# Seven block products for layer 0's output projection, and one norm chain for its four row blocks

## The chip, the cores and the metric

The kernel runs on one core of a Trainium2 chip. The core has a matrix engine (TensorE, PE in the profile), a vector engine (VectorE, DVE), a scalar engine (ScalarE, ACT), GpSimd (POOL) and a queue of transfers issued by SyncE (SP). Each engine works through its own instructions in order; semaphores order them against each other. TensorE writes to PSUM[...].

The metric is the device time of one execution in microseconds, the median of several runs. Lower is better.

## The reference

The input x is 8 images of 512 channels and 32 x 32 = 1024 positions, all in float32. Two attention layers follow each other. Cut to what matters here, layer 0 is

```python
hn = group_norm(x, gn1_scale, gn1_bias)                  # 32 groups of 16 channels
qkv = einsum('bchw,oc->bohw', hn, w_qkv) + b_qkv
wgt = softmax((q * s).T @ (k * s))                       # 8 heads of 64 channels
a = einsum('bts,bcs->bct', wgt, v).reshape(b, c, h, w)
out = einsum('bchw,oc->bohw', a, w_proj) + b_proj        # the output projection
out = group_norm(out, gn2_scale, gn2_bias)
return x + out
```

Layer 1 takes this as its x: `qkv = w_qkv @ x` with row-normalized weights, divided by the root of its mean square over the channels, one-head attention over 1024 positions, an output matrix, and `(x + h) / sqrt(2)`.

## The kernel before, in words

**Tiles.** 512 channels are CI = 4 row blocks of 128 partitions, so an image is a tile of 4 x 1024 floats per partition. A matmul takes 128x128 weights and 128x512 moving data; the 1024 positions are two halves of 512 (HN). Seven buffers of one image's size ("slots") are handed out by name and given back (`big`, `slots.give`): x, the normed x, the values, the attention output `a`, the projected `o`, the turned probabilities `pT`. PSUM has three tiles of two banks (`wide`) and two of one bank (`bank`), used in turn.

**Order.** Every engine call goes through `InOrder`, which keeps the written order on each engine. The order of the work is thus that of the Python lines.

**A block** is one image. The loop `for b in range(B)` runs 32 softmax steps (4 pairs of heads, 8 query blocks). A step computes scores on TensorE, maximum and transpose on VectorE, exponentials on ScalarE, scaling on GpSimd, and moves the transposed probabilities into `pT` by four transfers on SP. TensorE fills its time with the projections of the next heads, and uses `pT` (`heads.values`) some steps later. `heads.turn` does the transpose and its four transfers.

**The end of the softmax** (lines 1003 to 1016). The next image's values (`project_v0`, 8 groups of 4 matmuls, handed out by `next(v0)`) are spread as filling: one group, the last values but one, the last transpose, `fetch("score", b)`, three groups, the last values, and then `finish_layer0`, which uses the other four groups.

**The projection and its norm** (`finish_layer0`, lines 527 to 584). For each row block j of the output and each half, 4 matmuls accumulate over the 4 row blocks of `a`: 32 matmuls. ScalarE writes the row with its bias to `o` (line 569). VectorE takes the statistics of each row (`bn_stats` twice, `bn_aggr`). `GroupNorm` averages them over groups of 16 channels by a small matmul with `gavg` (`pm`), subtracts, averages the variances by another (`pv`), takes an inverse root in 13 small VectorE steps (`rsqrt_steps`, line 190), and makes a scale `a` and an offset `c`. `apply` scales the row on ScalarE, `add` adds it to x on VectorE. Each row block has a chain of its own, staggered: rows are applied while later rows are projected, and the last two during v0's groups. The last block (`half`, `begun`) has half of the sums made during its softmax steps, since there is no next image to fill with.

**Layer 1** (`Layer1`) follows. `project` multiplies x by an upper triangular matrix `gram` (`py`, 20 matmuls; row cj needs rows 0 to cj of x), then `Seven` computes scores, values and weights. `Seven` (line 586) is a scheme of Strassen and Winograd: a product of 2 x 2 blocks from 7 block products in place of 8. Its left operands A11, A12, A22, S1 to S4 are blocks of the weights and sums of them, made once at the start and kept in DRAM (`far`); its right ones are blocks B of the data and sums T1 to T4 of them, which VectorE makes per block (`sum_x`). Two products share one PSUM tile and are drained together, mostly by additions on VectorE, into the four blocks of the result.

**Weights** do not all fit. They share three buffers, w_qk, w_v and w_p, and are fetched from DRAM anew in each block (`places`, `fetch`; SP's queue in written order): w_qk holds qk, then score; w_v holds v, then value; w_p holds proj, then gram. `fetch` waits until the readers of the former tenant are done. `prep_layer1` (line 899) makes the layer 1 weights and the transposed projection once, at the start.

Of the kernel before, what the change touches and what calls it, by code (L numbers as in the profile page):

```python
# [13 lines left out]
P = 128  # L14
# [38 lines left out]
def attention_blocks_kernel(  # L53
# [52 lines left out]
    def big(name, lead=CI):  # L106

        return slots.take([P, lead, CI * N // lead], name)
# [93 lines left out]
    def rsqrt(r, v, n, name):  # L202
# [300 lines left out]
    def out_terms(a, j, th, cis):  # L503
        hs = slice(th * HN, (th + 1) * HN)
        return [(near["proj"][:, ci, j * P : (j + 1) * P], a[:, ci, hs]) for ci in cis]
# [21 lines left out]
    def finish_layer0(b, h, xt, v0, o=None, begun=None):  # L527


        half = o is not None  # L530
        if not half:
            o = big(f"o_{b}")

        def project_out(j, th, pm):
            terms = out_terms(h.a, j, th, range(CI // 2, CI) if half else range(CI))
            if half and j in begun.pm:
                PE.matmul(pm[:, th, :], *terms[1], start=False, stop=True)
            else:
                run(matmuls(pm[:, th, :], terms))

        norms = {}

        def norm(j):
            st = small.tile([P, 2, 6], F32, tag="gn_st2", name=f"st2_{b}_{j}")
            mv = small.tile([P, 1, 2], F32, tag="gn_mv2", name=f"mv2_{b}_{j}")
            for k in range(2):
                gn_stats(st, o[:, j, :], k)
            VE.bn_aggr(mv[:, 0, :], st)
            norms[j] = GroupNorm(mv, 1, G2S + j, G2B + j, f"2_{b}_{j}")

        def apply(j):
            a, c = norms[j].coeffs()
            AC.activation(o[:, j, :], o[:, j, :], AF.Identity, bias=c, scale=a)

        def add(j):
            VE.tensor_add(xt[:, j, :], xt[:, j, :], o[:, j, :])

        for j in range(CI):
            pm = begun.pm[j] if half and j in begun.pm else wide(f"pp_{b}_{j}")
# [6 lines left out]
            if half:  # L566
                VE.tensor_add(o[:, j, :], o[:, j, :], pm.rearrange("p a f -> p (a f)"))
            else:
                AC.activation(o[:, j, :], pm.rearrange("p a f -> p (a f)"), AF.Identity, bias=col(BP, j))
# [5 lines left out]
        next(v0, None)  # L575
        fetch("gram", b)
        add(CI - 2)
        norms[CI - 1].means()
        next(v0, None)
        apply(CI - 1)  # L580
        add(CI - 1)
        run(v0)
        slots.give(f"a_{b}")
        slots.give(f"o_{b}")

    class Seven:

# [6 lines left out]

        half, drains = None, []

        def __init__(self, name, width, left, right, c, last, swap=False):
            self.name, self.width, self.left, self.right, self.swap = name, width, left, right, swap
            self.c, self.last = c, last

        def product(self, a, b, drain):
            first = Seven.half is None
# [22 lines left out]
        def steps(self):  # L625
            c, add, last = self.c, VE.tensor_add, self.last

            def c21(pm):
                add(c["21"], c["22"], pm)
                last("21")  # L630

            def both(pm):
                add(c["22"], c["22"], pm)
                last("22")
                add(c["12"], c["12"], pm)

            def c12(pm):
                add(c["12"], c["12"], pm)
                last("12")

            def c11(pm):
                add(c["11"], c["11"], pm)
                last("11")

            for a, b, drain in (
                (A11, "B11", lambda pm: AC.copy(c["11"], pm)),
                (S2, "T2", lambda pm: add(c["12"], c["11"], pm)),
                (S3, "T3", lambda pm: add(c["22"], c["12"], pm)),
                (A22, "T4", c21),
                (S1, "T1", both),  # L650
                (S4, "B22", c12),
                (A12, "B21", c11),
            ):
                self.product(a, b, drain)
                yield

    class Layer1:


# [1 line left out]

        def __init__(self, b, xt):
            self.b, self.xt = b, xt
            self.t12, self.t34 = (block.tile([P, 2, 2, HN], F32, tag="pb", name=f"t{k}_{b}") for k in (12, 34))
            self.e, self.sums = {}, {}

        def right(self, cols):

            first, second = cols, slice(HN + cols.start, HN + cols.stop)

            def operand(name, h):
                if name[0] == "B":
                    return self.xt[:, 2 * (name[1] == "2") + h, second if name[2] == "2" else first]
                tile_, k = {"T1": (self.t12, 0), "T2": (self.t12, 1), "T3": (self.t34, 0), "T4": (self.t34, 1)}[name]
                return tile_[:, k, h, cols]

            return operand

        def sum_x(self, j):

            xt, t12, t34 = self.xt, self.t12, self.t34
            m, (t1, t2) = j % 2, (slice(0, HN), slice(HN, N))
            if j < 2:
                VE.tensor_sub(t12[:, 0, m], xt[:, m, t2], xt[:, m, t1])
            else:
                VE.tensor_sub(t12[:, 1, m], xt[:, j, t2], t12[:, 0, m])
                VE.tensor_sub(t34[:, 0, m], xt[:, j, t2], xt[:, m, t2])
                VE.tensor_sub(t34[:, 1, m], xt[:, j, t1], t12[:, 1, m])

        def project(self):  # L690
            b, xt = self.b, self.xt
# [3 lines left out]
            for cj in range(CI):  # L695
                py = wide(f"py_{b}_{cj}")
                for th in range(2):
                    hs = slice(th * HN, (th + 1) * HN)
                    run(matmuls(py[:, th, :], [(near["gram"][:, ci, cj * P : (cj + 1) * P], xt[:, ci, hs]) for ci in range(cj + 1)]))
                self.sum_x(cj)  # L700
# [162 lines left out]
    PE.transpose(pcol, rows, ident[:NCOLS, :NCOLS])  # L863
    VE.tensor_copy(cols, pcol)
    VE.tensor_scalar_mul(bqs, cols[:, BQ : BQ + CI], QSCALE0)
    norm1.means()
    norm1.gn.coeffs()
    for ci in range(CI):
# [30 lines left out]
    def prep_layer1():  # L899
# [18 lines left out]
        for k, (name, w) in enumerate((("score", score), ("value", value))):  # L918
            pool, tag = ((block, "pb"), (prob, "p"))[k]
            s7 = [pool.tile([P, 4, 2, CH], F32, tag=tag, name=f"{name}7_{i}") for i in range(2)]  # L920
# [10 lines left out]
        done2 = big("done2", 2 * CI)  # L931
        gram, proj = done2[:, :CI, :], done2[:, CI:, :]

        VE.memset(gram, 0.0)
        for ci in range(CI):
# [8 lines left out]
        for name in ("w1_qk", "w1_vo", "rows_vp", "done1", "done2"):  # L944
            slots.give(name)
        fetch("proj", 0)

    prep_layer1()

# [5 lines left out]
    for b in range(B):  # L955
# [47 lines left out]
        v0 = iter(())  # L1003
        if more:
            v0_next = big(f"v0_{b + 1}", NT)
            v0 = project_v0(b + 1, hn_next, v0_next)
        next(v0, None)
        heads.values(STEPS // RG - 2)
        heads.turn()
        fetch("score", b)  # L1010
        for _ in range(3):
            next(v0, None)
# [63 lines left out]
```

## Time and profile before

| | us |
|---|---|
| median of 3 runs | 3366.11 |
| lowest, highest | 3365.45, 3367.4 |
| the profiled execution's own time | 3368.53 |
| its span, first to last instruction | 3366.4 |
| TensorE busy | 3310.3 (98%) |
| VectorE busy | 2093.1 (62%) |
| ScalarE busy | 1091.8 (32%) |
| GpSimd busy | 979.2 (29%) |
| mean granted TensorE clock | 0.996 of full |

The profile is one execution. Its views used here: the busy shares; the chain of work that ended last, followed back from the last instruction; the groups of instructions, with count, busy time, mean of one, and what ended the idle time before; the timeline of one engine; and windows, which give busy time of PE, PEld (weight loads), DVE, ACT, POOL, each with its number of records, then the granted clock of TensorE, the DMA share and GB/s for a stretch of time. Nearly every line of the kernel shows as L34, the helper that keeps the order, so groups are told apart by tile names: `pp` is the projection in PSUM, `pm` and `pv<-d,gavg` the norm's small matmuls, `pv<-v,hn` the next image's values, `py` the gram product, `p_u` layer 1's score products. A float32 matmul is two records.

### The profile page before, as it was taken

How to read it: one execution, taken by the hardware profiler on the slowest of the kernel's cores; microseconds unless marked ns; L12 is line 12 of the kernel's file. 1: busy time of each engine (PE TensorE's matmuls, PEld its weight loads, DVE VectorE, ACT ScalarE, POOL GpSimd, SP SyncE). 2: the span in 40 equal slices, each digit the busy share in tenths (PEclk: the TensorE clock that was granted, in tenths of full speed). 3: DMA queues.
4: the chain of work that ended last, by engine and by line, in shares of the span. 5: the costliest groups of instructions: out<-in, count | busy, mean ns of one | idle time of the engine just before them, and what ended most of it. 6: DMA issues, size and time to landing. Idle time of an engine off the chain costs nothing.

```text
span 3366.4 us, 36221 instructions
## 1 busy us (share of the span) xinstructions
PE 3310.3 (98%) x13329; PEld 1628.9 (48%) x13329; DVE 2093.1 (62%) x3175; ACT 1091.8 (32%) x1825; POOL 979.2 (29%) x852
## 2 busy tenths in 40 slices
PE   7999999999999999999999999999999999999799
PEld 3544544445444454444544445444454545444354
DVE  4595646956479454884449754596546956468653
ACT  2353123531145212451125412254123531145210
POOL 0253123521235112450224503254022521235111
PEclk9999999999999999999999999999999999999899
DMA  5486205752068410782118811287204852058500
GB/s 184 137 209 186 79 13 150 198 159 81 2 188 206 125 69 25 200 221 89 55 44 217 226 59 44 74 220 203 78 14 127 205 166 78 13 145 204 158 7 25
DMA packets 183239, 410.86 MB, mean 122 GB/s; under 512 B 27508, under 2 KB 27544, under 8 KB 176280
## 3 DMA queue, kind: packets, MB, share of 16 engines
q1 hardware_dynamic: 182944, 408.53, 42.8%
q8 instruction: 106, 1.74, 0.2%
q14 instruction: 69, 0.57, 0.1%
q10 hardware_dynamic: 120, 0.02, 0.0%
HBM read 114.32 MB, written 25.72 MB: 42 GB/s over the span
## 4 chain that ended last, share of the span: by engine, by line
PE 88%; DVE 7%; DMA 2%; ACT 1%; issue 1%; SPq 1%; DVEq 0%; ACTq 0%
PE po L34 26%; PE s L34 13%; PE pqk L34 13%; PE p_e_T L34 7%; PE p_e_B L34 5%; PE pv L34 5%; PE py L34 4%; PE pp L34 4%; PE p_u_T L34 3%; PE p_v_T L34 2%; PE p_u_B L34 2%; PE p_v_B L34 2%; DMA pT<-pb 2%; DVE s L34 1%; DVE rs L34 1%; DVE x L34 1%
## 5 line engine op out<-in xcount | busy, mean ns | idle before, releaser
L34 POOL TENSOR_SCALAR p<-p,tt 128x1024 f32<-128x1024 f32 x512 | 565.9, 1118 | 935.0 <-DVE tt L34 931.6
L34 ACT ACTIVATE p<-s,nm 128x1024 f32<-128x1024 f32 x512 | 565.5, 1109 | 839.9 <-DVE nm L34 800.2
L34 DVE TENSOR_REDUCE nm<-s 128x1 f32<-128x1024 f32 x512 | 602.3, 1218 | 174.4 <-PE s L34 173.7
L34 DVE STREAM_TRANSPOSE pb<-p 128x2048 f32<-128x2048 f32 x256 | 589.5, 2303 | 28.4 <-POOL p L34 18.7
L34 PE MATMUL s<-qk 64*128 64x512 f32 x2048 | 510.4, 602 | 0.0
L34 PE MATMUL po<-pT,v 128*64 128x256 f32 x4096 | 471.7, 383 | 3.7 <-DMA pT<-pb 3.3
L34 PE MATMUL pqk<-hn,qk 64*128 64x512 f32 (+1 forms) x2016 | 474.4, 591 | 0.0
L34 PE MATMUL po<-e,v 128*128 128x512 f32 x1024 | 450.8, 595 | 0.0
L34 PEld LDWEIGHTS po<-pT,v 128*64 128x64 f32 x4096 | 287.3, 137 | 216.9 <-ACT v L34 69.7
L34 PEld LDWEIGHTS pqk<-hn,qk 64*128 64x128 f32 (+1 forms) x2016 | 202.0, 187 | 252.1 <-issue 239.7
L34 POOL TENSOR_TENSOR u<-u,xy 128x512 f32<-128x512 f32 x64 | 79.0, 1273 | 817.9 <-DMA xy<-far_rinv 727.3
L34 PEld LDWEIGHTS po<-e,v 128*128 128x128 f32 x1024 | 192.2, 190 | 252.7 <-issue 245.5
L34 PEld LDWEIGHTS s<-qk 64*128 64x128 f32 x2048 | 194.6, 186 | 239.4 <-issue 234.5
L34 PE MATMUL pv<-v,hn 128*128 128x512 f32 x512 | 233.2, 604 | 1.4 <-ACT v L34 1.4
L34 PE MATMUL pp<-a,proj 128*128 128x512 f32 x480 | 217.4, 604 | 0.0
L34 DVE TENSOR_TENSOR e<-e,p_e_T 128x512 f32<-128x512 f32 x160 | 107.0, 685 | 145.0 <-PE p_e_T L34 142.8
L34 POOL TENSOR_TENSOR qk<-qk,v 128x512 f32<-128x512 f32 x124 | 158.2, 1276 | 84.2 <-ACT v L34 84.2
L34 ACT ACTIVATE e<-e,shift,rinv 128x512 f32<-128x512 f32 x128 | 100.9, 811 | 247.7 <-DVE e L34 247.7
L34 POOL TENSOR_TENSOR esum<-esum,e 128x512 f32<-128x512 f32 x96 | 121.5, 1267 | 163.9 <-ACT e L34 161.4
L34 PEld LDWEIGHTS pv<-v,hn 128*128 128x128 f32 x512 | 94.2, 191 | 111.2 <-issue 109.4
L34 PE MATMUL p_e_T<-s,t 128*128 128x512 f32 x320 | 147.8, 592 | 0.0
L34 DVE BATCH_NORM_STATS2 st<-o 128x6 f32<-128x512 f32 x64 | 41.0, 683 | 168.2 <-ACT o L34 168.2
(171 smaller groups left out, 3048.2 us busy)
## 6 DMA issues: line engine op xcount, KB each, us to landing
pT<-pb SPq DMA_DIRECT2D x1024, 256.0 KB, 4.5
hn<-in_x_dram SPq DMA_DIRECT2D x32, 512.0 KB, 5.8
x<-in_x_dram SPq DMA_DIRECT2D x32, 512.0 KB, 5.8
out_dram<-x SPq DMA_DIRECT2D x32, 512.0 KB, 3.9
score<-far_score SPq DMA_DIRECT2D x8, 1792.0 KB
value<-far_value SPq DMA_DIRECT2D x8, 1792.0 KB
qk<-far_qk SPq DMA_DIRECT2D x7, 2048.0 KB
proj<-far_proj SPq DMA_DIRECT2D x8, 1024.0 KB, 4.8
```

The costliest lines, as they stand in the source:

```text
L34: return lambda *args, **kw: self._pin(call(*args, **kw))
```

## The change

The output projection of the first seven blocks is computed by `Seven`: two units of 7 products, each product two matmuls, 28 in all. The weights' seven left operands are made in the set-up (`proj7`) and share the buffer w_qk with qk and score. `gram` stays in w_p from the start until the last block. The right operands' sums, formerly a method of `Layer1`, become a class `RightSide`, and are made for `a` in a slot of their own (`ta`): rows 0 to 2 ahead of the last values, row 3 after them. The bias is added in the drains of the first and the third product (`bpd` holds the difference of two biases). The statistics of all four rows go through one `GroupNorm` of width 4; rows are applied after it. The fetch of score moves behind the projection. The last block keeps its form under the name `finish_last`. In the set-up the transposition of the projection's weights moves ahead of the gram.

```diff
+    bpd = const.tile([P, 2], F32, name="bpd")
...
-        "proj": ("p", [P, CI, C]), "gram": ("p", [P, CI, C]),
+        "proj": ("p", [P, CI, C]), "gram": ("p", [P, CI, C]), "proj7": ("qk", [P, 7, 2, CH]),
...
+    class RightSide:
+        def __init__(self, xt, t12, t34):
+            self.xt, self.t12, self.t34 = xt, t12, t34
+
+        def sums(self, j):
+            xt, t12, t34 = self.xt, self.t12, self.t34
+            m, (t1, t2) = j % 2, (slice(0, HN), slice(HN, N))
+            if j < 2:
+                VE.tensor_sub(t12[:, 0, m], xt[:, m, t2], xt[:, m, t1])
+            else:
+                VE.tensor_sub(t12[:, 1, m], xt[:, j, t2], t12[:, 0, m])
+                VE.tensor_sub(t34[:, 0, m], xt[:, j, t2], xt[:, m, t2])
+                VE.tensor_sub(t34[:, 1, m], xt[:, j, t1], t12[:, 1, m])
...
     class Seven:
...
+            def c11_first(pm):
+                if self.bias:
+                    AC.activation(c["11"], pm, AF.Identity, bias=self.bias[0])
+                else:
+                    AC.copy(c["11"], pm)
+
+            def c22_first(pm):
+                if self.bias:
+                    VE.scalar_tensor_tensor(c["22"], pm, self.bias[1], c["12"], ALU.add, ALU.add)
+                else:
+                    add(c["22"], c["12"], pm)
...
             for a, b, drain in (
-                (A11, "B11", lambda pm: AC.copy(c["11"], pm)),
+                (A11, "B11", c11_first),
                 (S2, "T2", lambda pm: add(c["12"], c["11"], pm)),
-                (S3, "T3", lambda pm: add(c["22"], c["12"], pm)),
+                (S3, "T3", c22_first),
                 (A22, "T4", c21),
                 (S1, "T1", both),
                 (S4, "B22", c12),
...
+    def finish_layer0(b, h, rhs, xt, v0):
+        o, w = big(f"o_{b}"), near["proj7"]
+        st = small.tile([P, CI, 2, 6], F32, tag="gn_st2", name=f"st2_{b}")
+        mv = small.tile([P, CI, 2], F32, tag="gn_mv2", name=f"mv2_{b}")
+        norm = GroupNorm(mv, CI, G2S, G2B, f"2_{b}")
+
+        def unit(m):
+            c = {
+                f"{i + 1}{th + 1}": o[:, m + 2 * i, th * HN : (th + 1) * HN] for i in range(2) for th in range(2)
+            }
+            return Seven(
+                f"o_{b}_{m}", HN,
+                lambda k, hh: w[:, k, hh, m * P : (m + 1) * P], rhs.columns(slice(0, HN)), c, lambda which: None,
+                bias=(col(BP, m), bpd[:, m : m + 1]),
+            ).steps()
+
+        def stats(j):
+            for k in range(2):
+                gn_stats(st[:, j], o[:, j, :], k)
+
+        units = [unit(m) for m in range(2)]
+        for u in units:
+            next(u)
+
+        for j in range(CI // 2 + 1, CI):
+            rhs.sums(j)
+        for m, u in enumerate(units):
+            for k in range(6):
+                next(u)
+                if k == 3:
+                    stats(m + 2)
+            stats(m)
+        slots.give(f"a_{b}")
+        slots.give(f"ta_{b}")
+        fetch("score", b)
+        next(v0)
+        for j in range(CI):
+            VE.bn_aggr(mv[:, j, :], st[:, j])
+        norm.means()
+        next(v0)
+        a, c = norm.coeffs()
+        for j in range(CI):
+            AC.activation(o[:, j, :], o[:, j, :], AF.Identity, bias=c[:, j : j + 1], scale=a[:, j : j + 1])
+            VE.tensor_add(xt[:, j, :], xt[:, j, :], o[:, j, :])
+        run(v0)
+        slots.give(f"o_{b}")
...
-            if b + 1 < B:
+            if b + 1 == B - 1:
                 fetch("proj", b + 1)
...
+        for name, w, pool, tag in (("score", score, block, "pb"), ("value", value, prob, "p")):
+            operands(name, w, [pool.tile([P, 4, 2, CH], F32, tag=tag, name=f"{name}7_{i}") for i in range(2)])
+        slots.give("done1")
+        done2, done3 = big("done2", 2 * CI), big("done3", 2 * CI)
         gram, proj = done2[:, :CI, :], done2[:, CI:, :]
+        turn(wprow, proj, "p")
+        d3 = done3.rearrange("p (k h) c -> p k (h c)", k=2).rearrange("p k (i h c) -> p k i h c", h=2, c=CH)
+        operands("proj7", proj, [d3[:, k] for k in range(2)])
...
-        turn(wprow, proj, "p")
...
-        fetch("proj", 0)
+        fetch("gram", 0)
...
+            next(v0)
         heads.values(STEPS // RG - 2)
         heads.turn()
-        fetch("score", b)
-        for _ in range(3):
-            next(v0, None)
-        begun = None if more else OutBegun(b, heads)
+        if more:
+            fetch("proj7", b)
+            ta = big(f"ta_{b}").rearrange("p (k i) (h n) -> p k i h n", k=2, h=2)
+            rhs = RightSide(heads.a, ta[:, 0], ta[:, 1])
+            for j in range(CI // 2 + 1):
+                rhs.sums(j)
+            for _ in range(3):
+                next(v0)
+        else:
+            fetch("score", b)
+            begun = OutBegun(b, heads)
         heads.values(STEPS // RG - 1)
         slots.give(f"v0_{b}")
-        finish_layer0(b, heads, xt, v0, *(() if more else (o_last, begun)))
+        if more:
+            finish_layer0(b, heads, rhs, xt, v0)
+        else:
+            finish_last(b, heads, xt, o_last, begun)
```

`operands` is the code that made the seven left operands of score and value, now a function: four additions and subtractions on VectorE, three copies on GpSimd, two transfers to DRAM.

More of the change, by code (lines that the diff above doesn't have):

```diff
@@ L525, in __init__, with finish_last @@
                         PE.matmul(self.pm[j][:, th, :], lhsT, rhs, start=True, stop=False)
[L527 to L532, printed above, removed]
+    def finish_last(b, h, xt, o, begun):
         def project_out(j, th, pm):
-            terms = out_terms(h.a, j, th, range(CI // 2, CI) if half else range(CI))
-            if half and j in begun.pm:
+            terms = out_terms(h.a, j, th, range(CI // 2, CI))
+            if j in begun.pm:
                 PE.matmul(pm[:, th, :], *terms[1], start=False, stop=True)
@@ L558, in finish_layer0 @@
         for j in range(CI):
-            pm = begun.pm[j] if half and j in begun.pm else wide(f"pp_{b}_{j}")
+            pm = begun.pm[j] if j in begun.pm else wide(f"pp_{b}_{j}")
             project_out(j, 0, pm)
@@ L565, in finish_layer0 @@
                 add(j - 2)
[L566 to L569, printed above, removed]
+            VE.tensor_add(o[:, j, :], o[:, j, :], pm.rearrange("p a f -> p (a f)"))
             if j:
@@ L572, in finish_layer0 @@
             norm(j)
-        next(v0, None)
         apply(CI - 2)
-        next(v0, None)
         fetch("gram", b)
@@ L578, in finish_layer0, with columns, operand, __init__ @@
         norms[CI - 1].means()
-        next(v0, None)
         apply(CI - 1)
         add(CI - 1)
-        run(v0)
         slots.give(f"a_{b}")
         slots.give(f"o_{b}")
+    class RightSide:
[10 more added lines that the diff above has]
+                VE.tensor_sub(t34[:, 1, m], xt[:, j, t1], t12[:, 1, m])
+        def columns(self, cols):
+            first, second = cols, slice(HN + cols.start, HN + cols.stop)
+            def operand(name, h):
+                if name[0] == "B":
+                    return self.xt[:, 2 * (name[1] == "2") + h, second if name[2] == "2" else first]
+                tile_, k = {"T1": (self.t12, 0), "T2": (self.t12, 1), "T3": (self.t34, 0), "T4": (self.t34, 1)}[name]
+                return tile_[:, k, h, cols]
+            return operand
     class Seven:
         half, drains = None, []
-        def __init__(self, name, width, left, right, c, last, swap=False):
+        def __init__(self, name, width, left, right, c, last, swap=False, bias=None):
             self.name, self.width, self.left, self.right, self.swap = name, width, left, right, swap
-            self.c, self.last = c, last
+            self.c, self.last, self.bias = c, last, bias
         def product(self, a, b, drain):
@@ L663, in __init__ @@
             self.b, self.xt = b, xt
-            self.t12, self.t34 = (block.tile([P, 2, 2, HN], F32, tag="pb", name=f"t{k}_{b}") for k in (12, 34))
+            self.rhs = RightSide(xt, *(block.tile([P, 2, 2, HN], F32, tag="pb", name=f"t{k}_{b}") for k in (12, 34)))
+            self.right = self.rhs.columns
             self.e, self.sums = {}, {}
[L667 to L688, printed above, removed]
         def project(self):
@@ L699, in project @@
                     run(matmuls(py[:, th, :], [(near["gram"][:, ci, cj * P : (cj + 1) * P], xt[:, ci, hs]) for ci in range(cj + 1)]))
-                self.sum_x(cj)
+                self.rhs.sums(cj)
                 VE.tensor_mul(part if cj else acc, py.rearrange("p a f -> p (a f)"), xt[:, cj, :])
@@ L865, in attention_blocks_kernel @@
     VE.tensor_scalar_mul(bqs, cols[:, BQ : BQ + CI], QSCALE0)
+    VE.tensor_sub(bpd, cols[:, BP + 2 : BP + 4], cols[:, BP : BP + 2])
     norm1.means()
@@ L917, in prep_layer1, with operands @@
             AC.copy(value[:, ci, :], product(wv, [woT[:, o, :] for o in range(CI)], ci, 0, "pB"))
-        for k, (name, w) in enumerate((("score", score), ("value", value))):
-            pool, tag = ((block, "pb"), (prob, "p"))[k]
-            s7 = [pool.tile([P, 4, 2, CH], F32, tag=tag, name=f"{name}7_{i}") for i in range(2)]
+        def operands(name, w, s7):
             q = [[w[:, 2 * j : 2 * j + 2, i * CH : (i + 1) * CH] for j in range(2)] for i in range(2)]
@@ L930, in prep_layer1 @@
             SY.dma_start(out=far[name][:, 4:], in_=s7[1][:, :3])
-        done2 = big("done2", 2 * CI)
+        for name, w, pool, tag in (("score", score, block, "pb"), ("value", value, prob, "p")):
+            operands(name, w, [pool.tile([P, 4, 2, CH], F32, tag=tag, name=f"{name}7_{i}") for i in range(2)])
+        slots.give("done1")
+        done2, done3 = big("done2", 2 * CI), big("done3", 2 * CI)
         gram, proj = done2[:, :CI, :], done2[:, CI:, :]
+        turn(wprow, proj, "p")
+        d3 = done3.rearrange("p (k h) c -> p k (h c)", k=2).rearrange("p k (i h c) -> p k i h c", h=2, c=CH)
+        operands("proj7", proj, [d3[:, k] for k in range(2)])
         VE.memset(gram, 0.0)
@@ L940, in prep_layer1 @@
                 VE.tensor_scalar_mul(gram[:, ci, c0 + P :], pg[:, c0 + P :], 2.0)
-        turn(wprow, proj, "p")
         SY.dma_start(out=far["gram"], in_=gram)
         SY.dma_start(out=far["proj"], in_=proj)
-        for name in ("w1_qk", "w1_vo", "rows_vp", "done1", "done2"):
+        for name in ("w1_qk", "w1_vo", "rows_vp", "done2", "done3"):
             slots.give(name)
-        fetch("proj", 0)
+        fetch("gram", 0)
     prep_layer1()
@@ L1001, in attention_blocks_kernel @@
             heads.step(i, fill, early, later)
-        v0 = iter(())
         if more:
@@ L1006, in attention_blocks_kernel @@
             v0 = project_v0(b + 1, hn_next, v0_next)
-        next(v0, None)
+            next(v0)
         heads.values(STEPS // RG - 2)
         heads.turn()
-        fetch("score", b)
-        for _ in range(3):
-            next(v0, None)
-        begun = None if more else OutBegun(b, heads)
+        if more:
[9 more added lines that the diff above has]
+            begun = OutBegun(b, heads)
         heads.values(STEPS // RG - 1)
         slots.give(f"v0_{b}")
-        finish_layer0(b, heads, xt, v0, *(() if more else (o_last, begun)))
+        if more:
+            finish_layer0(b, heads, rhs, xt, v0)
+        else:
+            finish_last(b, heads, xt, o_last, begun)
         fetch("value", b)
```

## The prediction

> **What bounds the kernel now.** I read the page's busy shares and its chain first, then the groups, then TensorE's timeline around one output projection, then the load beside it. The first two name the bound:
>
> ```profile
> PE 3310.3 (98%) x13329; PEld 1628.9 (48%) x13329; DVE 2093.1 (62%) x3175; ACT 1091.8 (32%) x1825; POOL 979.2 (29%) x852
> PE 88%; DVE 7%; DMA 2%; ACT 1%; issue 1%; SPq 1%; DVEq 0%; ACTq 0%
> ```
>
> TensorE is busy 98% of the span and carries 88% of the chain. So a matmul that goes away is worth its time, if no engine makes TensorE wait in its place. These groups give the prices (behind the first bar: busy us and the mean ns of one record):
>
> ```profile
> L34 PE MATMUL pp<-a,proj 128*128 128x512 f32 x480 | 217.4, 604 | 0.0
> L34 DVE TENSOR_TENSOR u<-u,p_u_T 128x512 f32<-128x512 f32 x80 | 53.1, 680 | 43.6 <-PE p_u_T L34 42.5
> L34 DVE BATCH_NORM_STATS2 st<-o 128x6 f32<-128x512 f32 x64 | 41.0, 683 | 168.2 <-ACT o L34 168.2
> ```
>
> The 480 records of the projection are two per matmul (7 blocks x 32 + 16 in the last), and the 604 ns of a record overlap their neighbours. The true price comes from the timeline of TensorE, here block 1's projection and what follows (start, us, then the group):
>
> ```profile
> 725.51 14.00 PE L34 MATMUL pp<-a,proj 128*128 128x512 f32 x32
> 739.35 0.28 PE L34 MATMUL pm<-mv,gavg 128*128 128x1 f32 x2
> 739.49 3.68 PE L34 MATMUL pp<-a,proj 128*128 128x512 f32 x8
> 743.01 0.28 PE L34 MATMUL pv<-d,gavg 128*128 128x1 f32 x2
> ...
> 754.12 3.68 PE L34 MATMUL pv<-v,hn 128*128 128x512 f32 x8
> 757.92 0.38 PE L34 MATMUL pv<-d,gavg 128*128 128x1 f32 x2
> ...
> 765.71 0.38 PE L34 MATMUL pv<-d,gavg 128*128 128x1 f32 x2 [0.21 <-DVE d L34]
> 765.95 3.68 PE L34 MATMUL pv<-v,hn 128*128 128x512 f32 x8
> 769.47 17.33 PE L34 MATMUL py<-x,gram 128*128 128x512 f32 x40
> 786.63 1.88 PE L34 MATMUL p_u_B<-x,score 128*128 128x512 f32 x4
> ```
>
> The reader is to see three prices. **A matmul**: the 20 of py run from 769.47 to 786.63, 17.16 us, so 0.858 us each. **A small matmul of the norm**: from 739.49 to the next eight records of pp at 743.15 are 3.66 us, of which 4 x 0.858 = 3.43 are the big ones; 0.22 us remain. **The stage**: from the first pp to the first py 43.96 us here, and 43.69, 43.68, 43.68 and 43.68 us in the blocks at 319, 1131, 1942 and 2752 us; I take 43.7. It is made of 32 + 16 matmuls (4 groups of v0 follow the projection), 48 x 0.858 = 41.2; 8 small ones, 1.8; and 0.7 of waits for the norm, of which the row at 765.71 shows a piece.
>
> **The change, part by part.** All of it but the set-up falls into seven of the eight blocks; the last keeps its way.
>
> TensorE, per block. 28 product matmuls stand in place of 32: the new products have the form of layer 1's score products, which the rows show at 0.858 too (28 of them with a 1.7 us group between go from 786.63 to 812.45). One chain of the norm in place of four: 2 small matmuls for 8. New stage: 28 + 16 = 44 x 0.858 = 37.75; 2 x 0.22 = 0.44; waits, below, 0.1. Sum 38.3, so 5.4 us less per block: 3.4 from the products, 1.3 from small matmuls, 0.6 from waits.
>
> VectorE before the projection. The sums of rows 0 to 2 (5 subtractions, 0.60 us from start to start as in the rows of t<-x) are 3.1 us. VectorE did nothing from 709.95, its last transpose, to 733.83. They wait only until the values of the last group but one leave their buffer (711.4), and end near 714.6; nothing is queued behind them but the sums of row 3. Cost 0; without this cover they would cost 3.1.
>
> Row 3's sums come after the last values. Count from the end of these, 725.5 = 0: ScalarE writes row 3 by 0.6, the three subtractions end at 1.3, 1.9 and 2.5. The two first products (A11 x B11 of both units, no sums) keep TensorE until 3.43; the first use of a row-3 sum is at 4.3. Cover 3 us, cost 0.
>
> VectorE during the products: 3 sums, 14 drains (680 ns), 8 statistics (683 ns): 25 x 0.65 = 16 us within 24 us of TensorE. A pair of products takes 3.43 us, its drains at most 3 adds and 2 statistics, 3.3 us; three PSUM tiles rotate, so a pair may lag by two before TensorE waits. Cost 0. ScalarE drains two first products in place of four 128x1024 rows: less.
>
> The norm's tail is the one place where the change adds a wait. The products end at 24.0; I count anew from there. Two last adds to 1.3, two statistics to 2.6, four aggregates at 0.2 to 3.4. TensorE's first v0 group ends at 3.43, so the mean matmul waits 0 to 0.3; I take 0.1, since the steps of the trace start within 0.05 of their release. Mean and three small steps end at 4.7, while the second v0 group runs to 7.1. Then the variance matmul, 17 small steps of 0.194 (743.32 to 746.56 in block 1) to 10.7, ScalarE's row 1.24 to 12.0, the first add 1.22 to 13.2. The two last v0 groups hold TensorE until 4 x 3.43 + 0.44 + 0.1 = 14.3, when py wants row 0. Margin 1.1 us. Rows 1, 2, 3 are ready 1.2 us apart, py takes 1.7, 3.4 and 5.2 us per row. Cost 0; each us by which this chain is longer than counted past 1.1 costs 1 us per block. From above: if VectorE trails by a whole pair, 3 us, 1.9 us per block.
>
> Transfers. The proj7 load (1792 KB) stands on SP's queue where the score load stood, same size, same buffer, same release. What is new is that the projection needs it at once. Landing of the score load before (window of the DMA, last two columns DMA share and GB/s), in block 1 and in block 4, the tightest:
>
> ```profile
> 713.22 1.04 SPq L34 DMA_DIRECT2D score<-far_score  x1
> 722.50:723.00 0.50, 0.50 (x8) 0.33 (x6) 0.00 (x0) 0.50 (x1) 0.00 (x0) 1.00 0.07 29
> 723.00:723.50 0.50, 0.50 (x8) 0.31 (x6) 0.00 (x0) 0.03 (x1) 0.00 (x0) 1.00 0.00 0
> 1939.50:1940.00 0.50, 0.50 (x8) 0.29 (x6) 0.00 (x0) 0.00 (x0) 0.00 (x0) 1.00 0.19 61
> 1940.00:1940.50 0.50, 0.50 (x8) 0.34 (x6) 0.00 (x0) 0.00 (x0) 0.00 (x0) 1.00 0.00 0
> ```
>
> The last packets are in at 723.0 and 1940.0; the projection starts at 725.51 and 1941.84: 2.5 and 1.8 us to spare, 2.4 to 4.5 in the others. [...]By the row the cost is 0[...]; I take 0, and the range holds the rest. The score load moves behind the last product, at 24; alone it took 7 us in block 0 (307.6 to 315), so it lands near 32 and is read after py, at 24 + 14.3 + 17.2 = 55. On SP only the value load is queued behind its wait, and that waits for v0's end at 38 anyway. The gram load per block and seven of eight proj loads go; no TensorE wait hung on them: 0.
>
> Set-up, once: 4 VectorE and 3 GpSimd steps near 0.7 to 1.1 us, 1792 KB written, the 16 transposes moved ahead of the gram. VectorE was idle from 96 to 100 and from 101 to 108; with the steps it is ready near 103, and TensorE wants a bank back only at 110. Moved transposes: 1.8 us either way. The extra bias column on the start's chain: 0.2. Cost 0.2; without the cover 5.
>
> **Sum.** 7 x 5.4 = 37.8, less 0.2: 37.6. The profiled execution took 3368.5 us (span 3366.4 and 2.1 around it), 2.4 over the runs' median of 3366.1. It would come to 3330.9, the median to 3328.5.
>
> **Rivals.**
>
> The tail is longer: norm chain or load exposed by 1 to 4 us per block. For it: margins of 1.1 and 1.8 us. Against: both were counted from rows of the same forms. Time 3335 to 3356; at 2 us, 3342.
>
> Slower: proj7 lands late. A stall that long also costs clock. The last block shows it: TensorE idle for up to 5.8 us, and
>
> ```profile
> 3180.00:3185.00 5.00, 0.00 (x0) 0.00 (x0) 3.22 (x15) 1.24 (x1) 0.00 (x0) 0.50 0.32 135
> 3185.00:3190.00 5.00, 4.26 (x7) 2.20 (x8) 3.26 (x22) 0.31 (x1) 0.00 (x0) 0.50 0.00 0
> 3190.00:3195.00 5.00, 5.00 (x12) 2.17 (x12) 4.04 (x5) 0.93 (x1) 0.00 (x0) 0.96 0.00 0
> ```
>
> a granted clock of 0.50, and 19.4 us for the py that takes 17.2 elsewhere: 2.2 us more. [...]By the row a stall then costs itself and 2.2[...]; the gain of 5.4 is used up at 3.2[...] us.[...] The load would have to land 5 to 8 us later than the score load of the same size did in the same place. At 6 us late the time is 3328.5 + 7 x 8.2 = 3386.
>
> It does nothing: the gain comes back in a later stage, as where the softmax of blocks 3 and 4 waits for pT transfers (they stand on the chain at 1383 to 1421 and 1908 to 1923). Against: the waits of TensorE for pT come to 3.3 us in the whole span. Time 3360 to 3370.
>
> **How the numbers follow.** All hidden 0.85 (3325 to 3332); tail exposed 0.10; nothing 0.02; slower 0.03. Measurement tells 0.2% (6.7 us) from no change; below 3359.4 is faster: 0.95, same 0.02, slower 0.03. The range takes in the first case, 1 us per block more from fewer waits below and 1.7 us per block of exposed tail above: 3321 to 3340.
>
> **What would show it.** TensorE records of the output group fall by 7 x 8 = 56, small ones by 7 x 12 = 84. First product to first py: 38.3 us. Right: the first product starts with no wait for DMA, the clock stays at 1.00, and py starts with no wait for VectorE or 0.3 at most. Wrong: a wait of TensorE on proj7's load, or of py on x, times seven.

## The result, and the profile after

| | before | after |
|---|---|---|
| median, us | 3366.76 | 3327.27 |
| lowest, highest | 3365.45, 3368.5 | 3324.93, 3328.1 |
| the profiled execution, us | 3368.53 | 3326.53 |
| its span | 3366.4 | 3324.7 |
| mean granted TensorE clock | 0.996 | 0.997 |

After to before is 0.9881, with a 95% interval of 0.9864 to 0.9898: 39.5 us less, where 37.6 were forecast. Each median is of four runs.

The page of the kernel after, its busy shares and its chain:

```profile
PE 3270.4 (98%) x13189; PEld 1608.1 (48%) x13189; DVE 2127.5 (64%) x2893; ACT 1069.8 (32%) x1811; POOL 981.4 (30%) x855
PE 86%; DVE 6%; DMA 5%; SPq 2%; issue 1%; ACT 0%; DVEq 0%; POOL 0%; POOLq 0%; ACTq 0%
```

TensorE is 39.9 us less busy and still 98% busy, so the work that went was on the path and nothing has taken its place. The chain goes through transfers of `pT` more often than before (DMA 5% for 2%), but by the waits TensorE stood for them 2.6 us in the whole span, before 3.3. VectorE is busy for 34 us more, within its idle time.

The groups that took the place of `pp` (32 records of it remain, in the last block; after the bar: busy us, mean ns):

```profile
L34 PE MATMUL p_o_T<-ta,proj 128*128 128x512 f32 x224 | 98.4, 592 | 0.0
L34 PE MATMUL p_o_B<-a,proj 128*128 128x512 f32 x168 | 76.2, 596 | 0.0
L34 DVE SCALAR_TENSOR_TENSOR o<-p_o_T,bpd,o 128x512 f32<-128x512 f32 x14 | 10.5, 751 | 0.5
```

392 records are 7 blocks of 28 matmuls of two records. The drain that adds the bias takes 751 ns where a plain one takes 686.

TensorE's timeline of the stage in block 1:

```profile
717.18 3.70 PE L34 MATMUL p_o_B<-a,proj 128*128 128x512 f32 x8
720.72 7.03 PE L34 MATMUL p_o_T<-ta,proj 128*128 128x512 f32 x16
...
741.32 3.60 PE L34 MATMUL pv<-v,hn 128*128 128x512 f32 x8
744.75 0.28 PE L34 MATMUL pm<-mv,gavg 128*128 128x4 f32 x2
744.89 3.68 PE L34 MATMUL pv<-v,hn 128*128 128x512 f32 x8
748.41 0.28 PE L34 MATMUL pv<-d,gavg 128*128 128x4 f32 x2
748.55 7.11 PE L34 MATMUL pv<-v,hn 128*128 128x512 f32 x16
755.50 17.33 PE L34 MATMUL py<-x,gram 128*128 128x512 f32 x40
```

From the first product to the first `py` 755.50 - 717.18 = 38.32 us; before, 43.7. A bracket behind a row gives the idle time of the engine before it and what ended it. No row has one, so TensorE waits for nothing here, and each group starts where the one before it ends.

VectorE at the three places where something could have been late:

```profile
703.20 1.29 DVE L34 TENSOR_TENSOR ta<-a 128x512 f32<-128x512 f32 x2 [1.58 <-PE po L34]
...
719.02 0.68 DVE L34 TENSOR_TENSOR ta<-a,ta 128x512 f32<-128x512 f32 x1
...
741.52 1.28 DVE L34 TENSOR_TENSOR o<-o,p_o_B 128x512 f32<-128x512 f32 x2 [0.23 <-PE p_o_B L34]
...
753.38 4.63 DVE L34 TENSOR_TENSOR x<-x,o 128x1024 f32<-128x1024 f32 x4 [1.31 <-ACT o L34]
```

The first sums run 14 us ahead of the products; the last of row 3 ends at 719.70, 1.0 before 720.72, where the first matmul on `ta` starts. The last drains follow the last product within 0.2 us. The four adds to x take 4.63, so the first ends near 754.6, 0.9 before `py` wants its row.

The issue of the load of `proj7` on SP's queue:

```profile
705.19 0.83 SPq L34 DMA_DIRECT2D proj<-far_proj  x1
```

and two windows around its end (the last two columns are DMA share and GB/s):

```profile
713.50:714.00 0.50, 0.50 (x5) 0.34 (x6) 0.00 (x0) 0.32 (x1) 0.00 (x0) 1.00 0.07 29
714.00:714.50 0.50, 0.50 (x10) 0.29 (x5) 0.00 (x0) 0.50 (x1) 0.00 (x0) 1.00 0.00 0
```

Read as the prediction reads such windows, the last packets are in at 714.0, 3.2 us ahead of the first product, and 3.0 in block 4, the tightest before. The windows count a packet where it begins, though. In the packet records of the trace the last one of the load takes 0.54 us and ends at 714.27, so 2.9 us are left, 2.6 to 3.5 over the seven blocks. By the same count the score load had 2.2 us left before in block 1 and 1.5 in block 4, where the prediction read 2.5 and 1.8.

**Where the 41.7 us between the two spans come from.** The same group (24 `pv` before the last values) starts every 405.14 us in the undisturbed blocks before, every 399.79 after. By the stage (43.68 and 38.32) it is 5.36 per block, times seven 37.5. Another 1.8 are waits of irregular size that lengthened three of the blocks before (405.42, 405.77 and 406.03 in place of 405.14). The second trace of the kernel after, below, has such blocks too (400.24, 400.43 and 400.70 in place of 399.79), so this part is chance and not a gain. 2.1 us were gained before that group of block 0: 1.0 in an early load of weights (the same group starts 1.6 us apart in two executions of the kernel after, so the start moves by as much anyway); 0.6 in a score tile of block 0, below; 0.5 I can't assign. 0.3 is left for the end.

### The profile page after: what moved, and what is told of

The parts are those of the page before. It is cut to its first block, busy times and chain, and to the rows that moved or that the text cites. A ratio compares the mean times of both kernels' runs of the same rounds, so it can differ in the third digit from the quotient of the medians.

```text
span 3324.7 us, 35644 instructions
## 1 busy us (share of the span) xinstructions
PE 3270.4 (98%) x13189; PEld 1608.1 (48%) x13189; DVE 2127.5 (64%) x2893; ACT 1069.8 (32%) x1811; POOL 981.4 (30%) x855
## 4 chain that ended last, share of the span: by engine, by line
PE 86%; DVE 6%; DMA 5%; SPq 2%; issue 1%; ACT 0%; DVEq 0%; POOL 0%; POOLq 0%; ACTq 0%
PE po L34 24%; PE pqk L34 11%; PE s L34 11%; PE pv L34 7%; PE p_e_T L34 7%; PE p_e_B L34 5%; DMA pT<-pb 5%; PE py L34 4%; PE p_u_T L34 3%; PE p_o_T L34 3%; PE p_v_T L34 2%; PE p_u_B L34 2%; DVE pb L34 2%; PE p_o_B L34 2%; PE p_v_B L34 2%; SPq L34 2%
## 5 line engine op out<-in xcount | busy, mean ns | idle before, releaser
L34 DVE TENSOR_TENSOR v<-po,esum 128x512 f32<-128x512 f32 x56 | 38.7, 691 | 160.0 <-PE po L34 159.8
L34 PE MATMUL py<-x,gram 128*128 128x512 f32 x320 | 140.7, 599 | 0.0
```

The source lines that it names most:

```text
L34: return lambda *args, **kw: self._pin(call(*args, **kw))
```

## The experiments

**The kernel after once more**, beside the others as the measure for them.

> The changed kernel once more, beside the others, as their base: 3327 us, first product to first py 38.3 us in each of seven blocks.

Measured: 3327.82 us (3326.91 to 3330.11), ratio to the kernel before 0.9885 (0.987 to 0.9899). Differences below are to this.

**The chain without the products.** The kernel before, with one chain for the four rows in the first seven blocks; the eight block products stay.

```diff
...
+        fetch("gram", b)
+        next(v0)
+        for j in range(CI):
+            VE.bn_aggr(mv[:, j, :], st[:, j])
+        gn.means()
+        next(v0)
+        a, c = gn.coeffs()
+        for j in range(CI):
+            AC.activation(o[:, j, :], o[:, j, :], AF.Identity, bias=c[:, j : j + 1], scale=a[:, j : j + 1])
+            VE.tensor_add(xt[:, j, :], xt[:, j, :], o[:, j, :])
+        run(v0)
...
-        finish_layer0(b, heads, xt, v0, *(() if more else (o_last, begun)))
+        if more:
+            finish_one(b, heads, xt, v0)
```

> The kernel before with its eight block products, and one chain of the norm for the four row blocks in the first seven blocks. Theory: 48 x 0.858 + 0.44 + 0.1 = 41.7 us for the stage, 2.0 less than 43.7, so 14 us less than before: 3353 us. Rival (the chain was the bound): most of the gain appears here already, about 38.3 us for the stage and 3330 us. Rival (one chain only moves the wait to its end): stage 43 us or more, 3362 us or more.

Measured: 3353.58 (3350.06 to 3354.61), ratio 0.9959 (0.9945 to 0.9974). TensorE's timeline in block 1:

```profile
720.80 27.73 PE L34 MATMUL pp<-a,proj 128*128 128x512 f32 x64
...
762.55 17.33 PE L34 MATMUL py<-x,gram 128*128 128x512 f32 x40
```

The stage is 41.75 us. So the chain alone takes 43.7 - 41.75 = 1.95 off each block and the products another 41.75 - 38.32 = 3.43, which is 4 x 0.858 with nothing lost. In time: 13.1 us for the chain, 25.8 for the products given the chain.

**The products without the chain.** The kernel after, with a chain for each row; two of them are handed out between the second unit's products, as far as that is possible, two behind.

```diff
+                if m == 1:
+                    if k == 0:
+                        norms[2].means()
+                    elif k == 1:
+                        apply(2)
+                    elif k == 2:
+                        norms[0].means()
+                    elif k == 3:
+                        add(2)
+                    elif k == 4:
+                        apply(0)
...
         next(v0)
-        for j in range(CI):
-            VE.bn_aggr(mv[:, j, :], st[:, j])
-        norm.means()
+        norms[1].means()
+        add(0)
         next(v0)
...
```

> The seven products are kept; the norm goes back to four chains of one row block each, two of them run during the second unit and two during the next image's values. My theory (the gain is TensorE's own work: 3.4 us per block of products, 1.3 of small matmuls, 0.6 of waits): six small matmuls come back, 6 x 0.22 = 1.3 us per block and 0 to 1.4 us of waits, so 39.6 to 41 us from first product to py and 3337 to 3346 us. Rival (the four staggered chains bounded the stage, and the products are hidden beside them): the stage goes back to about 43.7 us and the time to 3365.

Measured: 3421.1 (3417.82 to 3423.95), ratio 1.016 (1.0145 to 1.0176). Far slower than either said, and slower than the kernel before. TensorE in block 1:

```profile
759.60 3.60 PE L34 MATMUL pv<-v,hn 128*128 128x512 f32 x8
767.78 0.38 PE L34 MATMUL pm<-mv,gavg 128*128 128x1 f32 x2 [4.58 <-DVE mv L34]
768.03 5.38 PE L34 MATMUL pv<-v,hn 128*128 128x512 f32 x8
...
780.03 0.38 PE L34 MATMUL pv<-d,gavg 128*128 128x1 f32 x2 [2.75 <-DVE d L34]
```

VectorE in the same stretch:

```profile
756.58 0.16 DVE L34 TENSOR_TENSOR c<-cols,c 128x1 f32<-128x1 f32 x1
...
757.30 2.00 DVE L34 TENSOR_TENSOR o<-o,p_o_T 128x512 f32<-128x512 f32 x3
...
764.89 1.28 DVE L34 TENSOR_TENSOR o<-o,p_o_B 128x512 f32<-128x512 f32 x2
```

The products end at 759.60, 25.25 us after their start (24.14 in the kernel after, which has no small matmuls among them), but their last drains start at 764.89; in the kernel after they follow at once. VectorE was never idle in between: the small steps of two chains and an add stand ahead of the drains in its queue. Those steps start 0.19 us apart (0.20 in the chain of four columns, which has as many steps as a chain of one). The statistics of the last row are late, TensorE waits 4.58 us for its mean, and the clock falls: the granted clock is 0.50 from 769 to 771, and the eight records behind the mean take 5.38 us for 3.68. The second wait, 2.75 us, is for the last chain, which is handed out behind the one before it.

Of the 93 us by which this run is slower than the kernel after, 51 are these two waits in seven blocks, and some 9 the six small matmuls (7 x 6 x 0.22). Most of the rest is clock: between first product and end of `py` it stands at 0.50 for 61 us in the seven blocks, which costs at most half of that, an estimate from the 0.50.

**The same with fewer small steps.** If the small steps make the lateness, leaving some out gives time back one for one. Two of the three rounds of the inverse root of layer 0's second norm are left out in the first seven blocks, eight steps per chain, so the scale is less exact there.

```diff
-        for _ in range(3):
+        for _ in range(rounds):
...
+            norms[j].few = True
```

> The run with seven products and four chains, with two of the three Newton steps of layer 0's second norm left out in the first seven blocks (8 small VectorE steps fewer per chain, so this norm is less exact than the reference's). Theory (VectorE is what four chains overload: its steps stand between the drains of the products): 4 x 8 x 0.194 = 6.2 us less VectorE per block, most of it on the path, and shorter idle stretches of TensorE, so 4 to 8 us per block off 3421: 3365 to 3393 us. Rival (the handing over between TensorE, VectorE and ScalarE sets the time, not the number of steps): under 2 us per block, 3407 us or more.

Measured: 3371.05 (3367.45 to 3373.05), ratio 1.0013 (1.0006 to 1.002). 50 us less, 7.15 per block, for 32 steps less per block, whose own time is 32 x 0.194 = 6.2; the rival said under 2. TensorE's waits, in the kernel with full chains (us, times, longest):

```profile
PE pm L34 <- DVE mv L34: 35.6, 9, 4.6
PE pv L34 <- DVE d L34: 34.5, 12, 5.8
```

and with the short ones:

```profile
PE pm L34 <- DVE mv L34: 16.1, 9, 1.9
PE pv L34 <- DVE d L34: 23.8, 12, 5.8
```

The wait for the last row's mean falls from 4.59 to 1.91 in each block (the 5.8 are of the last block, which keeps its four chains in both). The two lines fall by 30.2 us, 4.3 per block. The other 2.8 go with the clock: in the seven blocks it stands at 0.50 for 17 us in place of 61. So the number of small steps ahead of the drains sets the time, and a part of what it costs is paid in clock.

**Four chains, but behind the drains.** Place or number? All four are handed out after the last product, in the order in which `py` needs the rows. The diff is against the run with four chains among the drains.

```diff
-                if m == 1:
-                    if k == 0:
-                        norms[2].means()
...
         next(v0)
-        norms[1].means()
-        add(0)
+        for j in range(CI - 1):
+            norms[j].means()
         next(v0)
+        apply(0)
+        norms[CI - 1].means()
         apply(1)
+        add(0)
...
```

> Seven products and four chains, but no small step of a norm before the last drain: means and coefficients of all four rows behind the products. Theory (it is the chains among the drains that cost 94 us, and VectorE's 4 x 17 small steps that remain): the products run in 24 us as with one chain; behind them row 0 comes 2 us later than with one chain and rows 1 and 2 are late for py by 3 us each, 5 to 7 us per block over the changed kernel: 3362 to 3377 us. Rival (four chains cost the same wherever they stand): 3415 us or more.

Measured: 3355.92 (3353.06 to 3357.48), ratio 0.9967 (0.9956 to 0.9979). 65 us better than among the drains, 28 worse than one chain: 4.0 per block, under the 5 to 7 expected. TensorE in block 1:

```profile
762.84 2.84 PE L34 MATMUL py<-x,gram 128*128 128x512 f32 x6 [0.33 <-DVE x L34]
767.12 14.86 PE L34 MATMUL py<-x,gram 128*128 128x512 f32 x34 [1.44 <-DVE x L34]
```

The stage is 2.1 us longer, from small matmuls and small waits, and `py` 1.8, since the later rows of x come behind the later chains. I had counted too much of the chains as exposed: `py`'s first records run ahead of the second wait and cover a part of them.

So the place is worth 65 us, the clock that its stalls cost included, and the number 28. Of the two arrangements, seven products with four chains beat the kernel before only with the chains behind the drains, and then by 10 us, not 39. Two chains of two rows each were not run.

**Less cover for the norm's tail.** Four groups of v0 before the last values in place of three, so three are left behind the products.

```diff
-            for _ in range(3):
+            for _ in range(4):
                 next(v0)
```

> The changed kernel with one of the four groups of the next image's values that follow the products (3.43 us) moved ahead of the last values of the softmax: the same work, but only three groups to hide the norm's tail. Theory: the tail ends at 13.2 to 13.4 us behind the last product and the cover at 10.9, so py waits 2.3 to 2.5 us per block, 7 x 2.4 = 17 us: 3344 us. Rival (the tail is not on TensorE's path, py has other room): 3327 us.

Measured: 3347.64 (3346.01 to 3349.49), ratio 0.9947 (0.9932 to 0.9962). TensorE in block 1:

```profile
760.78 17.43 PE L34 MATMUL py<-x,gram 128*128 128x512 f32 x40 [2.43 <-DVE x L34]
```

A group is 3.43 us, and 2.43 show as a wait: the margin in the kernel after is 1.0. The time went up by 2.8 per block, 0.4 more than the wait; 0.1 of that is a longer `py`, the rest I can't assign.

**A late load.** The transfer of `proj7` is issued twice into the same tile.

```diff
             fetch("proj7", b)
+            SY.dma_start(out=near["proj7"], in_=far["proj7"])
```

> The changed kernel with the load of the projection's operands made twice in a row, so that it is complete some 7 us later. Theory (it is hidden by 3 to 4 us and no more): the second load is in near 721, the first product waits 3.5 to 4 us per block, 25 to 28 us, and [...]the clock falls and adds up to 2.2 us more per block: 3352 to 3370 us, about level with the kernel before. Rival (the load has far more room): 3327 us.

Measured: 3377.05 (3373.1 to 3382.22), ratio 1.0031 (1.0018 to 1.0045). TensorE in block 1:

```profile
729.34 5.36 PE L34 MATMUL p_o_B<-a,proj 128*128 128x512 f32 x8 [4.64 <-DMA proj<-far_proj]
```

The windows around its start (behind the five engines the granted clock, then DMA share and GB/s):

```profile
728.00:728.50 0.50, 0.00 (x0) 0.00 (x0) 0.00 (x0) 0.00 (x0) 0.00 (x0) 1.00 0.07 29
729.00:729.50 0.50, 0.16 (x1) 0.19 (x2) 0.00 (x0) 0.00 (x0) 0.00 (x0) 0.82 0.00 0
729.50:730.00 0.50, 0.50 (x1) 0.31 (x2) 0.00 (x0) 0.00 (x0) 0.00 (x0) 0.50 0.00 0
```

The waits come to 36.1 us in the seven blocks, 5.2 each. In each the granted clock falls to 0.50, and the eight records of the first product take 5.36 us for 3.70 here, 5.3 to 6.6 over the blocks. That is 1.6 to 2.9 us per block, 2.1 on the average and 14.9 in all. In blocks 0 to 2 the low clock lasts 3.4 us and costs 1.6 to 1.7, in blocks 3 to 6 it lasts 6.8 and costs 2.0 to 2.9. Waits and clock make 51 us; the medians are 49.2 apart, and the traced execution (3382.22) is the slowest of the five. I had expected a wait of 3.5 to 4, too little.

**The early sums taken away.** Rows 0 to 2 of `ta` are written behind the last values.

```diff
-        for j in range(CI // 2 + 1, CI):
+        for j in range(CI):
             rhs.sums(j)
...
-            for j in range(CI // 2 + 1):
-                rhs.sums(j)
```

> The changed kernel with the five sums of rows 0 to 2 made behind the last values, not while the softmax drains. By the sentence of the prediction (they cost 3.1 us without that cover): 7 x 3.1 = 22 us more, 3349 us. By a closer walk: the eight subtractions start 0.05 us behind the values and run 0.6 us apart, the first sums needed are the fourth and seventh, at 2.5 and 4.3 us where TensorE wants them at 3.4 and 4.3, so 0 to 0.3 us per block, 3327 to 3329 us.

Measured: 3327.9 (3326.5 to 3329.25), ratio 0.9887 (0.987 to 0.9903). It tells nothing about the cover: VectorE's first sums still start as soon as `a` is there, since moved as they are, nothing stands ahead of them in its queue.

```profile
703.05 1.29 DVE L34 TENSOR_TENSOR ta<-a 128x512 f32<-128x512 f32 x2 [1.58 <-PE po L34]
```

**The sums truly held.** The same, with a one-column copy of row 3 of `a` on VectorE ahead of all of them.

```diff
+        held = small.tile([P, 1], F32, tag="nmax0", name=f"held_{b}")
+        VE.tensor_copy(held, h.a[:, CI - 1, N - 1 : N])
-        for j in range(CI // 2 + 1, CI):
+        for j in range(CI):
             rhs.sums(j)
```

> All eight sums behind the last values in truth: one VectorE copy of the last column of row 3 stands ahead of them in VectorE's queue, so that they can't start while the softmax drains. By the sentence of the prediction (3.1 us per block without the cover): 7 x 3.1 = 22 us more, 3349 us. By the walk along the queue: sums from 0.85 us on, 0.6 us apart; the sixth is in at 4.5 us and TensorE wants it at 4.3, the others are in time, so 0.2 to 0.4 us per block: 3329 to 3331 us.

Measured: 3328.92 (3327.59 to 3330.96), ratio 0.9889 (0.9873 to 0.9906). VectorE in block 1:

```profile
717.82 0.15 DVE L34 COPY held<-a 128x1 f32<-128x1 f32 x1 [16.00 <-ACT a L34]
717.89 1.28 DVE L34 TENSOR_TENSOR ta<-a 128x512 f32<-128x512 f32 x2
```

TensorE behind it:

```profile
720.73 7.18 PE L34 MATMUL p_o_T<-ta,proj 128*128 128x512 f32 x16
```

Now no sum starts before 717.89, the last ends at 722.79, and the products on `ta` take 7.18 in place of 7.03: 0.15 per block, 1 us in all. Making the sums ahead, while the softmax drains, is worth next to nothing here: the two products on plain blocks of `a` that go first cover nearly all of it.

**One chain in the last block too.** It has no v0 groups to hide a chain under, so four chains stand one behind the other in front of `py`.

```diff
+        norm = GroupNorm(mv, CI, G2S, G2B, f"2_{b}")
         for j in range(CI):
...
-            norm(j)
-        apply(CI - 2)
         fetch("gram", b)
-        add(CI - 2)
-        norms[CI - 1].means()
-        apply(CI - 1)
-        add(CI - 1)
+        for j in range(CI):
+            VE.bn_aggr(mv[:, j, :], st[:, j])
+        norm.means()
+        a, c = norm.coeffs()
+        for j in range(CI):
+            AC.activation(o[:, j, :], o[:, j, :], AF.Identity, bias=c[:, j : j + 1], scale=a[:, j : j + 1])
+            VE.tensor_add(xt[:, j, :], xt[:, j, :], o[:, j, :])
```

> The changed kernel, and one chain of the norm in the last block too, where four chains follow each other on VectorE without a next image to hide them. Four additions and four pairs of statistics from 3113.9 take 10 us, aggregates and small matmuls 2.4, 17 small steps 3.4, the first row on ScalarE and its addition 2.5: py at about 3132 where it stands at 3144.5 now, 12 us less: 3315 us. If the idle time there is not the chains but the clock or the gram load, nothing changes: 3327 us.

Measured: 3315.71 (3313.92 to 3318.45), ratio 0.9848 (0.9834 to 0.9863): 12.1 us below the kernel after, and the fastest here. Some of the waits of TensorE in the last block of the kernel after:

```profile
3127.35 0.59 PE L34 MATMUL pv<-d,gavg 128*128 128x1 f32 x2 [5.21 <-DVE d L34]
...
3144.00 0.58 PE L34 MATMUL pv<-d,gavg 128*128 128x1 f32 x2 [5.76 <-DVE d L34]
3144.45 19.36 PE L34 MATMUL py<-x,gram 128*128 128x512 f32 x40
```

and all that is left of them with one chain:

```profile
3122.90 0.39 PE L34 MATMUL pm<-mv,gavg 128*128 128x4 f32 x2 [3.42 <-DVE mv L34]
3124.13 0.59 PE L34 MATMUL pv<-d,gavg 128*128 128x4 f32 x2 [0.84 <-DVE d L34]
3130.72 20.47 PE L34 MATMUL py<-x,gram 128*128 128x512 f32 x40 [6.01 <-DVE x L34]
```

From the first `pp` of 12 to `py` 42.8 us become 30.0, and `py` gives 1.1 back, since it follows a wait of 6 us directly: by the windows the granted clock is 0.50 for the first 6.2 us of it, for 3.9 in the kernel after.

## Why the prediction was right

**The bound and the price of a matmul: right.** TensorE's time fell by what left it. 38.3 us were forecast for the stage and 38.32 came. The parts hold one by one: the products 3.43 (forecast 3.4), and the chain 1.95 (1.3 of small matmuls and 0.6 of waits), each shown alone by the kernel with eight products and one chain. Records fell by 56 and 84 as written: 480 to 392 + 32, and 160 to 76.

**The norm's tail: right.** Forecast margin 1.1; the timeline shows 0.9, taking away a group of v0 shows 1.0. The rival of an exposed tail is real and was near: one group less costs 20 us.

**The load: right in sign, its margin mis-sized.** 1.8 to 2.5 us forecast in blocks 4 and 1, 3.0 and 3.2 measured. It was read from the score load in the same place. In block 1 that was issued 12.3 us ahead of the projection and in after 9.8; the new one is issued 12.0 ahead and in after 8.8 (both by the windows). Between the last packet and the matmul there is a little more: where the load was made late, its last packet ended at 728.90 by the packet records, and the waiting matmul started at 729.34, 0.44 us later.

**The slower rival: the mechanism and the price right.** "By the row a stall then costs itself and 2.2". The late load cost itself and 2.1 on the average; that this mean of 1.6 to 2.9 comes so near to 2.2 is in part luck. Three of the blocks paid 1.6 to 1.7, the other four 2.0 to 2.9, since the clock stayed low for 6.8 us there and not for 3.4. With a gain of 5.4 to 5.6 per block the load may be 3.3 to 3.5 us late before the change loses, an estimate from these numbers, where the prediction has 3.2. At 5.2 late it lost by 0.3%. The prediction speaks of the clock for long stalls only, of up to 5.8 us; here it fell after stalls of 1.91 us too (last section).

**Row 0 to 2's sums: "Cost 0; without this cover they would cost 3.1": the second half is wrong.** It took the sums' own length for their price. Held back until the last row was there, they cost 0.15 per block. The step that I failed to carry over stands one paragraph further on in the prediction: the two first products use no sums and keep TensorE for 3.4 us. The next product reads T2, whose last piece is the sixth of the eight sums; held back, that ends near 721.6 (720.29 and 1.29), and TensorE gets to it at 721.6 as well, one matmul of 0.858 after 720.73. Row 3's own sums came as forecast: the first ends 1.3 us after the products' start, 3.1 ahead of its use.

**The set-up: forecast at +0.2, too small to tell.** One part shows: block 0's first score tile waited for a PSUM bank that the last transposes of the set-up held. Its second half starts at 118.20, behind ScalarE's copy of them (117.56 to 118.14):

```profile
117.60 2.58 PE L34 MATMUL s<-qk 64*128 64x512 f32 x8
```

before, and after, with the transposes moved ahead of the gram:

```profile
116.60 1.99 PE L34 MATMUL s<-qk 64*128 64x512 f32 x8
```

0.6 us less. "Moved transposes: 1.8 us either way" counted TensorE's time and not who holds the bank behind them. The sum of the set-up stays open: block 0's first product starts at 319.48 and 317.58 in the two traces with the old set-up, and between 315.78 and 319.17 in eight with the new one.

**What the prediction did not say.** It took the one chain as a small saving beside the products, 1.9 of 5.4. The runs show it to be what makes the products pay in full. Eight block products are drained by ScalarE; seven are drained mostly by VectorE, and a chain per row among those drains holds up VectorE's queue: 54 us slower than before. With the four chains behind the drains the products gain 10. Nothing in the sum was wrong by this, since both came together; a reader who took the parts as independent would have been.

## What to carry to other kernels

When a scheme trades matmuls for additions, look at what else stands in the queue of the engine that makes the additions: chains of small dependent steps among its drains hold the drains up. Among the drains they cost 65 us more than behind them here, where the saved matmuls are worth 26. Merge such chains over rows, since a step of four columns costs what one of one column does (0.20 and 0.19 us here), put the chain behind the last drain, and count in matmul groups what covers its tail. An operand that is made early is worth its time only if nothing ahead of its first reader covers it already: here it was worth 0.15 us per block.

## What was not expected of the hardware

**Which stalls cost clock.** The length of a stall of TensorE does not decide alone whether the clock falls. In the run with fewer small steps it waits 1.91 us at the same place in each of seven blocks. In five of them the granted clock is 0.50 for the next 3.4 us, in two it stays at 1.00. Blocks 1 and 3:

```profile
754.37 0.38 PE L34 MATMUL pm<-mv,gavg 128*128 128x1 f32 x2 [1.91 <-DVE mv L34]
754.62 5.38 PE L34 MATMUL pv<-v,hn 128*128 128x512 f32 x8
...
1568.07 0.38 PE L34 MATMUL pm<-mv,gavg 128*128 128x1 f32 x2 [1.91 <-DVE mv L34]
1568.32 3.68 PE L34 MATMUL pv<-v,hn 128*128 128x512 f32 x8
```

The windows in which most of those eight records run (the granted clock is the third number from the end):

```profile
755.00:758.40 3.40, 3.40 (x5) 1.35 (x4) 1.60 (x4) 0.00 (x0) 0.00 (x0) 0.50 0.03 13
1567.35:1570.75 3.40, 2.68 (x8) 1.47 (x9) 2.41 (x7) 0.00 (x0) 0.00 (x0) 1.00 0.42 177
```

The stage takes 45.2 us in the five blocks and 43.5 in the two, so one such stretch of low clock costs 1.7.

Longer stalls did not always cost clock either. In block 1 of the run with less cover the clock stayed at 1.00 behind the 2.43 us, and the mean granted clock of that trace is 0.996, of the kernel after 0.997. Of the seven stalls of 2.75 us (the second wait with four chains among the drains), the eight records behind took 6.5 to 6.7 us in three and 3.68 in four.

The changes of the clock keep to steps. In the traces of the kernel before and after it stands at 0.50 for 3.41, 6.83 and 13.65 us, and at 1.00 for 3.41 and 23.89 us between these: 1, 2, 4 and 7 times 3.4133, and the 174.08 us at 1.00 behind the last are 51 times that. Counted in such steps from 755.00, where it falls in block 1 above, the stall of block 1 lies whole within one (751.59 to 755.00), that of block 3 is cut in two at 1567.37. Whether this place decides, two stalls do not show; no run here moves a stall and leaves the rest as it is.

**Small steps.** VectorE's dependent steps on 128 x 1 and on 128 x 4 elements start 0.19 and 0.20 us apart: the width is free, the count is not.
